# Normalising the second attention's first inputs early, and applying its norm weight to the input instead of the weights

## Chip, cores and metric

The kernel runs on one core of a Trainium2 chip. The metric is the device time of one launch in microseconds (us), as the median of several executions. One more execution was recorded by the hardware profiler. Engines are TensorE (PE, with its weight loads PEld), VectorE (DVE), ScalarE (ACT), GpSimd (POOL) and SyncE (SP), which issues the DMAs. They run in parallel, each of them in its own program order, and wait for one another through semaphores.

## The reference

All data is fp32: 16 batches of 512 positions with 512 features. Three blocks follow one another for each batch: a cross-attention with 16 heads over 77 keys and a norm behind it, a mamba2 block with a residual (its output is `h`), and a second cross-attention with 8 heads of 64 over the same 77 context rows and a norm before it. The change is in the last one:

```python
h = _mamba2_block(x, ...)
xn = (h - mean(h)) * rsqrt(var(h) + EPS) * ln_w + ln_b     # per row of 512
q = (xn @ Wq).reshape(b, Lq, 8, 64)
k, v = enc @ Wk, enc @ Wv                                   # 77 keys
p = softmax(where(pad_mask, -1e9, q k^T / 8))
out = h + (p @ v) @ Wo
```

`ln_w` and `ln_b` are vectors of 512, neither constant nor zero in the data.

## The kernel before, in words

**Stages.** The keys and values of both attentions are made first. Then PhaseA does the first attention of all batches, PhaseB the mamba blocks and PhaseC the second attention. Results between stages lie in DRAM. PhaseB has 8 units of work a batch (n = 128, one for each 128 of the 1024 inner channels) and PhaseC 4 (n = 64, one for each pair of heads). The last drain of PhaseB (`rest`, five units) is interleaved with PhaseC's weights (`setup`) and its first units (`lead`, units -14 to -1) in `tile_kernel`, L1590 to L1615.

**Order.** Each engine's order is that of the program text: PE, DVE, ACT and POOL are scheduled by hand all through, SP inside PhaseB's units. Every unit is a list of steps in which each step works for a unit some lags ahead or behind, so that a step's input has been made some units earlier. In PhaseC (`unit`, L1444) a lag of -5 means: for the unit five later.

**Precision.** A full-precision product is three matmuls (`mm3`, L36 to L38) on operands split into a rounded high part and the rest: names end in h and l. Splitting is one cast on ACT and one subtraction on another engine.

**PhaseB around the change.** `prepare` (L873) normalises, transposes and stores the next batch's input, within the units of the current one; the last batch has no next one. `turn_x1` (L856) is the DVE block transpose. The tiles for this (tag x8, two buffers) are thus free in the last batch.

**PhaseC, one unit.** In the order of the text: `turn_p` (L1406, DVE block transpose `pb` of the probabilities, then a DMA), `finish` (L1439, DVE adds the residual: `hr`), `soft_exp` (L1384, eight ACT exponentials), `qproj` (PE, 12 matmuls), `scores` (L1370, four matmuls; DVE adds the padding, `sc`, and takes the maximum, `mx`), `soft_div` (L1390: DVE reciprocal `sm`, POOL product `sc`), `query` (L1366, ACT moves `q` out of PSUM and adds the bias `bq`), `load_xT` (DMA of transposed input `xf`), `split_x` (L1353, ACT cast `nh`, POOL subtraction `nl`), in two of four units `norm` (L1332, two ACT activations `ht`) and `turn_x` (L1337, two DVE transposes `xb`), in another one `store_x` (L1343), `stats` (L1319, DVE mean and variance of one row block), in one of four units `rstd` (L1327: 12 small DVE operations `c_ve`, `c_y`, `c_t`, then two on POOL, `nm`), `attend` (L1416, PE; ACT cast `ct1h`, DVE subtraction `ct1l`), `project` (PE). So `h` is loaded 14 units ahead, normalised 9 ahead, stored transposed to DRAM, loaded back 6 ahead and split 5 ahead.

**The norm's weight and bias** are put into the query weights once: `setup` (L1264) loads Wq, computes `bq` = ln_b Wq with 16 matmuls of one column, scales Wq's rows by ln_w on DVE (L1292), and splits Wq; then Wo is split in four pieces (`split_piece` L126, `stream` L145), one in `setup` and three while the first units run.

```python
def split_x(self, b, k):
    xf = self.XF.pop((b, k))
    xh, xl = self.X[b, k] = pair(self.p1, [P, S], "n", bufs=8)
    self.nc.scalar.copy(xh, xf)
    self.nc.gpsimd.tensor_sub(xl, xf, xh.bitcast(F32))
```

Of the kernel before, what the change touches and what calls it, by code (L numbers as in the profile page):

```python
# [8 lines left out]
F32 = mybir.dt.float32  # L9
FR = mybir.dt.float32r  # L10
U8 = mybir.dt.uint8
AF = mybir.ActivationFunctionType
# [706 lines left out]
class PhaseB:  # L719


    def __init__(self, g):
        self.g, self.nc = g, g.nc
        self.n = 8 * g.nb
        self.drain = False
        self.Bt, self.Ut = {}, {}
        seq = []
        for i in range(self.n):
            if i % 8 == 0 and i == 0:
                seq += [16, 17]  # L730
            seq += [8 + i % 8, i % 8]
            if i % 8 == 7 and i + 1 < self.n:
                seq += [16, 17]
        self.wseq = iter(seq)
        self.wq = []
# [137 lines left out]
    def prepare(self, b, step):  # L873

        if step in (1, 2):
            self.scale_x1((0, 1) if step == 1 else (2, 3))
        if step in (2, 3):
            for m in (0, 1) if step == 2 else (2, 3):
                self.turn_x1(m)
        if step == 4:  # L880
            self.store_x1(b)
        if step == 5:
            self.load_xT(b)

    def head_x(self, b, k):
        nc, o = self.nc, self.Bt[b]
# [247 lines left out]
    def unit(self, i, side=iter(())):  # L1134


        n, nb = self.n, self.g.nb
        cur, prev, prev2 = (divmod(i - q, 8) if 0 <= i - q < n else None for q in range(3))

        def tail(lag):  # L1140
            b, q = divmod(i - lag, 8)
            return (b, q % 4, q >= 4) if i >= lag and b < nb else (0, 0, None)

        tb, tm, late = tail(6)
        eb, em, elate = tail(7)
        nxt = i // 8 + 1 if i % 8 == 7 and i // 8 + 1 < nb else None
        first = cur and cur[1] == 0
        more = i // 8 + 1 if i // 8 + 1 < nb else None
        k = i % 8
        if more and k == 0:  # L1150
            self.load_x1(more)
        if prev:
            self.tokens(*prev)
        if nxt:
            self.head_turn(nxt)
        if elate:
            self.tail_end(eb, em)
        if prev2:
            self.gate(*prev2)
        if prev:  # L1160
            self.weigh(*prev)
            self.decay(*prev)
        if cur:
            self.projx(*cur)
            if i:
                self.load_decay(*cur)
            self.convx(*cur)
        if i == 0:
            self.head_decay(0)
            self.store_decay(0)  # L1170
            self.load_decay(0, 0)
        next(side, None)
        if nxt:
            self.head_steps(nxt)
        if elate:
            self.tail_store(eb, em)
        if prev:
            self.steps(*prev)
        if nxt:
            self.projz(*cur)  # L1180
            self.head_x(nxt, 2)
            self.head_x(nxt, 3)
        next(side, None)
        if late is not None:
            self.Bt[tb].ps = self.out_half(tb, tm, 4 * late)
        if first:
            self.head_silu(cur[0])
        if late is False:
            part = self.o2.tile([P, D], F32, name="part", bufs=4)
            self.nc.scalar.copy(part, self.Bt[tb].ps)  # L1190
            self.Bt[tb].part.append(part)
        if prev:
            self.states(*prev)
        if k == 2 and i >= 10:
            self.tail_norm(i // 8 - 1)
        if late:
            self.tail_pre(tb, tm)
        if prev2:
            self.gate_split(*prev2)
        if cur:  # L1200
            self.silux(*cur)
            if not nxt:
                self.projz(*cur)
        if prev:
            self.load_ecs(*prev)
        if first:
            self.head_bt(cur[0])
        next(side, None)
        if prev:
            self.intra(*prev)  # L1210
        if more and k in (1, 2, 3, 4, 5):
            self.prepare(more, k)
        if nxt:
            self.head_bc(nxt, 0)
        next(side, None)
        if first:
            self.head_g(cur[0])
        if prev:
            self.inter(*prev)
        if more and k == 6:  # L1220
            self.head_dt(more)
            self.head_x(more, 0)
            self.head_x(more, 1)
        if nxt:
            self.head_decay(nxt)
            self.head_bc(nxt, 1)
            self.store_decay(nxt)
        lb, lm, llate = tail(5)
        if llate:
            self.tail_load(lb, lm)  # L1230
# [8 lines left out]
class PhaseC:  # L1239
# [24 lines left out]
    def setup(self):  # L1264

        g, nc, wp = self.g, self.nc, self.wp
        nc.scalar.preload_act_table_set("natural_log_exp_and_others")
        lw = wp.tile([P, KT], F32, name="lw")
        nc.sync.dma_start(lw, col_view(g.i["L1_ca_ln_w"]))
        lb = wp.tile([P, KT], F32, name="lb")  # L1270
        nc.sync.dma_start(lb, col_view(g.i["L1_ca_ln_b"]))
        self.kb = [wp.tile([P, KT, 2 * NK], F32, name=f"kc{j}") for j in range(2)]
        for j in range(2):
            nc.gpsimd.memset(self.kb[j], 0.0)
        self.padb = wp.tile([P, NK], F32, name="padb")
        nc.gpsimd.tensor_scalar(self.padb, g.padf, -1e9, 0.0, op0=ALU.mult, op1=ALU.add)
        self.wq = pair(wp, [P, KT, 512], "wq1")
        self.wo = pair(wp, [P, KT, 512], "wo1")
        self.bq = wp.tile([P, KT], F32, name="bq1")
        raws = [self.p1.tile([P, 512], F32, name="wr", bufs=6) for k in range(KT)]  # L1280
        for k in range(KT):
            nc.sync.dma_start(raws[k], g.i["L1_Wq"][k * P:(k + 1) * P, :])
        yield
        pbq = bank(g, "w")
        for t in range(KT):
            for k in range(KT):
                nc.tensor.matmul(pbq[:, t:t + 1], raws[k][:, t * P:(t + 1) * P], lb[:, k:k + 1],
                                 start=k == 0, stop=k == KT - 1)
        yield
        nc.vector.tensor_copy(self.bq, pbq[:, :KT])  # L1290
        for k in range(KT):
            nc.vector.tensor_scalar(raws[k], raws[k], lw[:, k:k + 1], None, op0=ALU.mult)  # L1292
            if k % 2:
                yield
        for k in range(KT):
            nc.scalar.copy(self.wq[0][:, k, :], raws[k])
            nc.vector.tensor_sub(self.wq[1][:, k, :], raws[k], self.wq[0][:, k, :].bitcast(F32))
            if k % 2:
                yield
        pieces = [split_piece(g, *self.wo, k, g.i["L1_Wo"], (self.p1, "wr", 6)) for k in range(KT)]  # L1300
        for _ in stream(pieces, 2):
            yield

    def load_h(self, b, m):
# [46 lines left out]
        self.nc.sync.dma_start(t_, self.g.xt1[b % 2][k * P:(k + 1) * P, :])  # L1351

    def split_x(self, b, k):  # L1353
        xf = self.XF.pop((b, k))
        xh, xl = self.X[b, k] = pair(self.p1, [P, S], "n", bufs=8)
        self.nc.scalar.copy(xh, xf)
        self.nc.gpsimd.tensor_sub(xl, xf, xh.bitcast(F32))

    def qproj(self, b, t):
        nc, wq = self.nc, self.wq  # L1360
# [4 lines left out]

    def query(self, b, t):  # L1366
        q = self.Q[b, t] = self.p1.tile([P, S], F32, name="q1")
        self.nc.scalar.activation(q, self.QP.pop((b, t)), AF.Identity, bias=self.bq[:, t:t + 1])

    def scores(self, b, t):  # L1370
        nc, q, kb = self.nc, self.Q.pop((b, t)), self.kb[b % 2]
# [72 lines left out]
    def unit(self, i):  # L1444


        def at(lag, f, *a):
            if 0 <= i - lag < self.n:
                f(*divmod(i - lag, 4), *a)

        last = i - 3 >= self.n - 2
        at(-14, self.load_h)
        if i % 4 == 1:
            at(-3, lambda b, t: self.load_k(b))
        if i % 4 == 0:
# [11 lines left out]
        at(-5, self.split_x)  # L1467
        if i % 4 in (3, 0):
            for m in (0, 1) if i % 4 == 3 else (2, 3):
                at(-9, lambda b, t: self.norm(b, m))  # L1470
                at(-9, lambda b, t: self.turn_x(b, m))
        if i % 4 == 1:
            at(-7, lambda b, t: self.store_x(b))
        at(-13, self.stats)
        if i % 4 == 2:
            at(-10, lambda b, t: self.rstd(b))
        at(4, self.attend)
        at(8, self.project)

    def lead(self):  # L1480
        for i in range(-14, 0):
            self.unit(i)
            yield

# [9 lines left out]
def tile_kernel(ctx: ExitStack, tc, ins, out, phases="kabc", dbg=None):  # L1494
# [28 lines left out]
    ctx.enter_context(tc.manual_schedule(engines={E.PE, E.DVE, E.Activation, E.Pool}))  # L1523
    nc.scalar.preload_act_table_set("natural_log_exp_and_others")
    A, B, C = PhaseA(g) if "a" in phases else None, PhaseB(g), PhaseC(g)

    def consts():
        nc.sync.dma_start(pad8, bcast_rows(ins["pad"][0]))
# [61 lines left out]
    if "c" in phases:  # L1590
# [4 lines left out]
            for _ in range(n):  # L1595
                next(it, None)

        step(lead, 3)
        step(setup)
        step(lead, 2)  # L1600
        step(rest)
        step(lead, 2)
        step(rest)
        for _ in range(3):
            step(setup, 2)
            step(rest)
            step(lead)
        step(lead, 4)
    for _ in rest:
        pass  # L1610
    if "b" in phases:
# [43 lines left out]
```

## Time and profile before

| what | value |
|---|---|
| median of 3 runs | 3018.6 us (3016.53 to 3019.37) |
| profiled execution | 3013.72 us, its span 3011.9 us |
| busy: PE / DVE / ACT / POOL | 2867.6 / 2406.4 / 1825.5 / 1473.1 us |
| share of the span | 95% / 80% / 61% / 49% |
| granted PE clock, mean | 0.985 |
| DMA, HBM read and written | 445.10 MB and 129.42 MB, 191 GB/s |
| last mamba batch | 2346 to 2446 us |
| transition: drain, setup, first units | 2446 to 2555 us |
| second attention | from 2498.42 us (first `sc`) to the end |

An engine's busy time is the sum of its instructions. A row of the timeline gives start, duration, engine, line, operation, output<-input and count, and in brackets the engine's idle time before it with what ended that. A row of the waits gives waiting operation <- what it waited for, the sum in us, how often, and the longest one. Starts of successive rows tell what an instruction costs its engine; durations overlap a little.

### The profile page before, as it was taken

How to read it: one execution, taken by the hardware profiler on the slowest of the kernel's cores; microseconds unless marked ns; L12 is line 12 of the kernel's file. 1: busy time of each engine (PE TensorE's matmuls, PEld its weight loads, DVE VectorE, ACT ScalarE, POOL GpSimd, SP SyncE). 2: the span in 40 equal slices, each digit the busy share in tenths (PEclk: the TensorE clock that was granted, in tenths of full speed). 3: DMA queues.
4: the chain of work that ended last, by engine and by line, in shares of the span. 5: the costliest groups of instructions: out<-in, count | busy, mean ns of one | idle time of the engine just before them, and what ended most of it. 6: DMA issues, size and time to landing. Idle time of an engine off the chain costs nothing.

```text
span 3011.9 us, 47659 instructions
## 1 busy us (share of the span) xinstructions
PE 2867.6 (95%) x15712; PEld 2144.9 (71%) x15712; DVE 2406.4 (80%) x3875; ACT 1825.5 (61%) x4970; POOL 1473.1 (49%) x1106
## 2 busy tenths in 40 slices
PE   9999999997799999999999999999999988999999
PEld 7755555554677877877787787778778765777776
DVE  4267888887878988988898898889889887777764
ACT  3256666664665666566666656666665647666663
POOL 1036666665665555555555555555555543333331
PEclk9999999998899999999999999999999988999999
DMA  7345555545566756665665666566566557989874
GB/s 231 92 125 156 164 161 155 158 143 155 172 195 193 224 164 203 213 183 191 195 222 167 202 210 186 188 197 220 171 202 206 169 177 217 267 271 274 269 242 149
DMA packets 421604, 578.22 MB, mean 192 GB/s; under 512 B 105982, under 2 KB 248494, under 8 KB 421358
## 3 DMA queue, kind: packets, MB, share of 16 engines
q1 hardware_dynamic: 421358, 575.18, 62.6%
q8 instruction: 125, 2.05, 0.3%
q14 instruction: 121, 0.99, 0.1%
HBM read 445.10 MB, written 129.42 MB: 191 GB/s over the span
## 4 chain that ended last, share of the span: by engine, by line
PE 53%; DVE 30%; issue 5%; POOL 4%; DMA 4%; ACT 2%; SPq 1%; DVEq 0%; POOLq 0%; ACTq 0%
DVE dbc L1016 6%; PE ps_o L36 5%; PE ps_o L38 5%; PE ps_o L37 5%; PE ps_w L37 4%; DVE dbc L1018 4%; DVE acc L815 4%; PE ps_w L38 4%; PE ps_w L36 4%; PE ps_y L36 3%; PE ps_y L37 3%; PE ps_y L38 3%; POOL nl L889 3%; PE ps_z L1074 2%; DVE sc L360 2%
## 5 line engine op out<-in xcount | busy, mean ns | idle before, releaser
L36 PE MATMUL ps_w<-nh,wb 128*128 128x512 f32 x1152 | 476.5, 414 | 0.3 <-ACT nh L888 0.3
L37 PE MATMUL ps_w<-nl,wb 128*128 128x512 f32 x1152 | 454.6, 395 | 15.9 <-POOL nl L889 15.9
L38 PE MATMUL ps_w<-nh,wb 128*128 128x512 f32 x1152 | 453.3, 394 | 0.0
L1083 POOL TENSOR_TENSOR yt<-yt,ebc 128x384 f32<-128x384 f32 x128 | 225.5, 1762 | 422.8 <-DVE ebc L1082 422.8
L1016 DVE TENSOR_TENSOR_SCAN dbc<-dbc,delta 128x512 f32<-128x512 f32 x256 | 387.0, 1554 | 0.0
L815 DVE SCALAR_TENSOR_TENSOR acc<-ps_w,cw,acc 128x511 f32<-128x511 f32 (+2 forms) x384 | 286.1, 745 | 23.4 <-ACT acc L813 14.4
L1018 DVE TENSOR_TENSOR dbc<-dbc,gm 128x1024 f32<-128x1024 f32 x128 | 272.1, 2125 | 5.5
L37 PEld LDWEIGHTS ps_w<-nl,wb 128*128 128x128 f32 x1152 | 218.3, 189 | 64.8 <-POOL nl L889 28.2
L1090 POOL TENSOR_TENSOR gl<-yt,gh 128x512 fp32r<-128x512 f32 x128 | 170.5, 1332 | 185.9 <-ACT gh L1089 180.2
L1084 POOL TENSOR_TENSOR yt<-yt,sz 128x512 f32<-128x512 f32 x128 | 254.9, 1991 | 10.0
L38 PEld LDWEIGHTS ps_w<-nh,wb 128*128 128x128 f32 x1152 | 216.9, 188 | 47.8
L36 PEld LDWEIGHTS ps_w<-nh,wb 128*128 128x128 f32 x1152 | 218.1, 189 | 41.1 <-issue 2.6
L1393 POOL TENSOR_TENSOR sc<-sc,sm 128x616 f32<-128x616 f32 x64 | 78.6, 1229 | 295.3 <-DVE sm L1392 263.9
L1044 ACT ACTIVATE u<-ps_x,dt 128x64 f32<-128x64 f32 x1024 | 221.9, 333 | 0.0
L1035 ACT ACTIVATE wu<-ps_x,et 128x64 f32<-128x64 f32 x768 | 170.9, 323 | 68.6 <-PE ps_x L1026 68.6
L813 ACT ACTIVATE acc<-ps_w,cb,cw 128x512 f32<-128x512 f32 x128 | 99.8, 780 | 176.7 <-PE ps_w L38 176.7
L360 DVE TENSOR_TENSOR sc<-ps_s,mt 77x2048 f32<-77x2048 f32 x64 | 145.1, 2267 | 71.8 <-PE ps_s L358 71.5
L36 PE MATMUL ps_o<-woph,gh 128*128 128x512 f32 x496 | 196.4, 396 | 0.0
L37 PE MATMUL ps_o<-wopl,gh 128*128 128x512 f32 x496 | 196.2, 396 | 0.0
L38 PE MATMUL ps_o<-woph,gl 128*128 128x512 f32 x496 | 196.2, 396 | 0.0
L1388 ACT ACTIVATE sc<-sc,mx 128x77 f32<-128x77 f32 x512 | 176.7, 352 | 0.2 <-DVE mx L1381 0.2
L889 POOL TENSOR_TENSOR nl<-xf,nh 128x512 fp32r<-128x512 f32 x64 | 101.0, 1600 | 125.4 <-ACT nh L888 125.4
(331 smaller groups left out, 7414.4 us busy)
## 6 DMA issues: line engine op xcount, KB each, us to landing
wb<-win SPq DMA_DIRECT2D x288, 512.0 KB
dbc<-dec SPq DMA_DIRECT2D x128, 512.0 KB
ebc<-ecs SPq DMA_DIRECT2D x256, 96.0 KB
pt<-pb SPq DMA_DIRECT2D x62, 384.0 KB
xt<-in_xT_dram SPq DMA_DIRECT2D x64, 256.0 KB
xb<-in_x_dram SPq DMA_DIRECT2D x64, 256.0 KB
x<-xb SPq DMA_DIRECT2D x64, 256.0 KB
xf<-x1t SPq DMA_DIRECT2D x16, 1024.0 KB
```

The costliest lines, as they stand in the source:

```text
L36: nc.tensor.matmul(ps, ah, bh, start=start, stop=False)
L37: nc.tensor.matmul(ps, ah, bl, start=False, stop=False)
L38: nc.tensor.matmul(ps, al, bh, start=False, stop=stop)
L360: nc.vector.tensor_mul(sc, ps[:NK], mt[:, None, :].to_broadcast((NK, 4, S)))
L815: nc.vector.scalar_tensor_tensor(acc[:, s:], ps[:, :S - s], cw[:, j, 3 - s:4 - s], acc[:, s:], op0=ALU.mult, op1=ALU.add)
L889: nc.gpsimd.tensor_sub(hl, o.xf[:, k, :], hh.bitcast(F32))
L1016: nc.vector.tensor_tensor_scan(flat, flat, self.delta.rearrange("p c i -> p (c i)"), 0.0, op0=ALU.mult, op1=ALU.add)
L1018: nc.vector.tensor_mul(lm, lm, o.gm[:, None, :, :].to_broadcast((P, 2, 4, P)))
L1044: nc.scalar.activation(w.u[:, c, h, :], w.pu[:, f:f + 64], AF.Copy, scale=o.dtc[:, c, 2 * t + h:2 * t + h + 1])
L1083: nc.gpsimd.tensor_add(yt[:, P:], yt[:, P:], t2)
L1084: nc.gpsimd.tensor_mul(yt, yt, w.sz)
L1388: self.nc.scalar.activation(sc[:, h, :], sc[:, h, :], AF.Exp, bias=mx[:, h:h + 1], accum_out=sm[:, h:h + 1])
```

## The change

**Early batches.** A new function `next_stage` of PhaseB is called nine times in the last mamba batch (units 120 to 128), for batches 0 and 1 of the second attention: it loads the whole `h` of the batch (1 MB), makes mean and variance on DVE (4 + 4 operations), the reciprocal deviation (12 small DVE operations, 2 on POOL), normalises on ACT (4), transposes on DVE (4), and stores by four DMAs to the place where `store_x` would. PhaseC leaves these steps out for its first 8 units (`done = 8`), and `lead` starts at unit -6 instead of -14.

**Weight and bias.** Wq is no longer scaled and there is no `bq`; Wq and Wo are split alike in a stream of eight pieces with four loads ahead (four pieces in the transition, four with the first units). Instead `split_x` multiplies each loaded `xf` by ln_w and adds ln_b in place, before the split, on DVE for batch 0 and on POOL for the other 15. `query` becomes a plain ACT copy.

**Order.** `setup`, `lead` and `rest` are interleaved anew, with SP's order by hand there too.

```diff
+    def next_stage(self, k):
+        g, nc, p2 = self.g, self.nc, self.p2
+        b, k = divmod(k, 4)
+        if k == 0 and b > 0:
+            x = self.XB.rearrange("p j m r -> p j (m r)")
+            dst = g.xt1[b - 1].rearrange("(j s) (a n) -> a s j n", s=32, n=P)
+            for a in range(4):
+                nc.sync.dma_start(dst[a], x[32 * a:32 * a + 32])
+        if b == 2:
+            return
+        if k == 0:
+            self.XN = p2.tile([P, KT, D], F32, name="xn", tag="x8")
+            nc.sync.dma_start(self.XN, g.h[b].rearrange("(m p) d -> p m d", p=P))
+        if k == 1:
+            self.HM = p2.tile([P, KT, 2], F32, name="hm", bufs=1)
+            for m in range(KT):
+                s6 = p2.tile([P, 6], F32, name="hs")
+                nc.vector.bn_stats(s6, self.XN[:, m, :])
+                nc.vector.bn_aggr(self.HM[:, m, :], s6)
+        if k == 2:
+            rs = rstd_bits(g, p2, self.HM[:, :, 1], [P, KT], "h")
+            nm = neg_mean(g, p2, self.HM[:, :, 0], rs, [P, KT], "hn")
+            for m in range(KT):
+                x = self.XN[:, m, :]
+                nc.scalar.activation(x, x, AF.Identity, scale=rs[:, m:m + 1], bias=nm[:, m:m + 1])
+        if k == 3:
+            for m in range(KT):
+                self.turn_x1(m)
...
+        if self.ahead and 0 <= i - n + 8 <= 8:
+            self.next_stage(i - n + 8)
...
-        pbq = bank(g, "w")
-        for t in range(KT):
-            for k in range(KT):
-                nc.tensor.matmul(pbq[:, t:t + 1], raws[k][:, t * P:(t + 1) * P], lb[:, k:k + 1],
-                                 start=k == 0, stop=k == KT - 1)
...
-            nc.vector.tensor_scalar(raws[k], raws[k], lw[:, k:k + 1], None, op0=ALU.mult)
...
+        pieces = [split_piece(g, *w, k, g.i[n], (self.p1, "wr", 6))
+                  for w, n in ((self.wq, "L1_Wq"), (self.wo, "L1_Wo")) for k in range(KT)]
+        for _ in stream(pieces, 4):
             yield
...
     def split_x(self, b, k):
-        xf = self.XF.pop((b, k))
+        nc, xf = self.nc, self.XF.pop((b, k))
         xh, xl = self.X[b, k] = pair(self.p1, [P, S], "n", bufs=8)
-        self.nc.scalar.copy(xh, xf)
-        self.nc.gpsimd.tensor_sub(xl, xf, xh.bitcast(F32))
+        e = nc.gpsimd if b else nc.vector
+        e.tensor_scalar(xf, xf, self.lw[:, k:k + 1], self.lb[:, k:k + 1], op0=ALU.mult, op1=ALU.add)
+        nc.scalar.copy(xh, xf)
+        nc.gpsimd.tensor_sub(xl, xf, xh.bitcast(F32))
...
-        self.nc.scalar.activation(q, self.QP.pop((b, t)), AF.Identity, bias=self.bq[:, t:t + 1])
+        self.nc.scalar.copy(q, self.QP.pop((b, t)))
...
-        at(-14, self.load_h)
+        todo(-14, self.load_h)
...
-        at(-13, self.stats)
+        todo(-13, self.stats)
...
-        for i in range(-14, 0):
+        for i in range(self.done and -6 or -14, 0):
...
-        step(lead, 3)
-        step(setup)
-        step(lead, 2)
-        step(rest)
-        step(lead, 2)
-        step(rest)
-        for _ in range(3):
+        with tc.manual_schedule(engines={E.SP}):
+            step(setup)
+            step(lead)
+            step(rest)
+            step(setup)
+            step(lead)
+            step(rest)
             step(setup, 2)
+            step(lead)
             step(rest)
             step(lead)
-        step(lead, 4)
+            step(lead)
+            step(rest)
+            step(lead)
+            step(rest)
+            step(lead, 14)
```

More of the change, by code (lines that the diff above doesn't have):

```diff
@@ L726, in __init__ @@
         self.Bt, self.Ut = {}, {}
+        self.ahead = False
         seq = []
@@ L1267, in setup @@
         nc.scalar.preload_act_table_set("natural_log_exp_and_others")
[L1268 to L1271, printed above, removed]
+        self.lw = wp.tile([P, KT], F32, name="lw")
+        nc.sync.dma_start(self.lw, col_view(g.i["L1_ca_ln_w"]))
+        self.lb = wp.tile([P, KT], F32, name="lb")
+        nc.sync.dma_start(self.lb, col_view(g.i["L1_ca_ln_b"]))
         self.kb = [wp.tile([P, KT, 2 * NK], F32, name=f"kc{j}") for j in range(2)]
@@ L1278, in setup @@
         self.wo = pair(wp, [P, KT, 512], "wo1")
-        self.bq = wp.tile([P, KT], F32, name="bq1")
-        raws = [self.p1.tile([P, 512], F32, name="wr", bufs=6) for k in range(KT)]
-        for k in range(KT):
-            nc.sync.dma_start(raws[k], g.i["L1_Wq"][k * P:(k + 1) * P, :])
-        yield
-        pbq = bank(g, "w")
-        for t in range(KT):
-            for k in range(KT):
-                nc.tensor.matmul(pbq[:, t:t + 1], raws[k][:, t * P:(t + 1) * P], lb[:, k:k + 1],
-                                 start=k == 0, stop=k == KT - 1)
-        yield
-        nc.vector.tensor_copy(self.bq, pbq[:, :KT])
-        for k in range(KT):
-            nc.vector.tensor_scalar(raws[k], raws[k], lw[:, k:k + 1], None, op0=ALU.mult)
[L1293 to L1301, printed above, removed]
+        pieces = [split_piece(g, *w, k, g.i[n], (self.p1, "wr", 6))
+                  for w, n in ((self.wq, "L1_Wq"), (self.wo, "L1_Wo")) for k in range(KT)]
+        for _ in stream(pieces, 4):
             yield
@@ L1449, in at, with todo @@
                 f(*divmod(i - lag, 4), *a)
+        def todo(lag, f, *a):
+            if i - lag >= self.done:
+                at(lag, f, *a)
         last = i - 3 >= self.n - 2
-        at(-14, self.load_h)
+        todo(-14, self.load_h)
         if i % 4 == 1:
@@ L1469, in unit @@
             for m in (0, 1) if i % 4 == 3 else (2, 3):
-                at(-9, lambda b, t: self.norm(b, m))
-                at(-9, lambda b, t: self.turn_x(b, m))
+                todo(-9, lambda b, t: self.norm(b, m))
+                todo(-9, lambda b, t: self.turn_x(b, m))
         if i % 4 == 1:
-            at(-7, lambda b, t: self.store_x(b))
-        at(-13, self.stats)
+            todo(-7, lambda b, t: self.store_x(b))
+        todo(-13, self.stats)
         if i % 4 == 2:
-            at(-10, lambda b, t: self.rstd(b))
+            todo(-10, lambda b, t: self.rstd(b))
         at(4, self.attend)
@@ L1525, in tile_kernel @@
     A, B, C = PhaseA(g) if "a" in phases else None, PhaseB(g), PhaseC(g)
+    B.ahead = "b" in phases and "c" in phases
+    C.done = 8 if B.ahead else 0
     def consts():
```

## The prediction

> **What bounds the kernel now.** The page puts TensorE (PE) at 95% of a span of 3011.9 us, but that is an average over stages, so I read the windows by stage first (columns: length, then busy time of PE, weight loads, DVE, ACT, POOL; granted PE clock; DMA share).
>
> ```profile
> 2346.00:2446.00 100.00, 96.17 (x597) 79.70 (x596) 91.63 (x128) 59.39 (x181) 57.38 (x35) 1.00 0.55 176
> 2446.00:2555.00 109.00, 83.49 (x338) 62.11 (x337) 86.24 (x207) 62.75 (x205) 37.76 (x44) 0.83 0.68 206
> 2555.00:2900.00 345.00, 345.00 (x1596) 255.76 (x1594) 268.81 (x571) 230.47 (x882) 113.45 (x110) 1.00 0.90 268
> ```
>
> Last mamba batch: PE 96% and DVE 92%, so both are nearly full. Transition: PE idle for 25.5 us of 109. Second attention: PE never idle, DVE 78%, POOL 33%. The waits between 2560 and 2950 show what order POOL, ACT and DVE stand in there:
>
> ```profile
> POOL sc L1393 <- DVE sm L1392: 206.7, 44, 5.3
> ACT q L1368 <- PE ps_y L38: 103.4, 48, 2.5
> DVE sc L1378 <- PE ps_w L1377: 77.0, 39, 2.6
> ```
>
> POOL's `sc` is always released by DVE's reciprocal; DVE's `sc` by PE. ACT's `nh` (L1356) waits only 8.2 us in all, for its DMA: today nothing that DVE or POOL makes is read by it. One unit (7.81 us of PE) with a normalisation in it, on DVE, ACT and POOL:
>
> ```profile
> 2641.36 1.01 DVE L1378 TENSOR_TENSOR sc<-ps_w,padb 128x308 f32<-128x308 f32 x2 [0.17 <-PE ps_w L1377]
> ...
> 2643.12 0.20 DVE L1392 RECIPROCAL sm<-sm 128x8 f32<-128x8 f32 x1
> 2643.23 1.26 DVE L94 STREAM_TRANSPOSE xb<-ht 128x512 f32<-128x512 f32 x2
> ...
> 2645.19 0.66 DVE L1425 TENSOR_TENSOR ct1l<-ps_z,ct1h 128x512 fp32r<-128x512 f32 x1
> 2645.76 0.97 DVE L94 STREAM_TRANSPOSE pb<-sc 128x768 f32<-128x768 f32 x1
> 2646.66 0.65 DVE L1441 TENSOR_TENSOR hr<-ps_o,hr 128x512 f32<-128x512 f32 x1
> 2649.17 1.00 DVE L1378 TENSOR_TENSOR sc<-ps_w,padb 128x308 f32<-128x308 f32 x2 [1.86 <-PE ps_w L1377]
> ```
>
> ```profile
> 2641.49 0.61 ACT L1356 CAST nh<-xf 128x512 fp32r<-128x512 f32 x1
> 2641.99 1.52 ACT L1335 ACTIVATE ht<-ht,nm,c_y 128x512 f32<-128x512 f32 x2
> 2643.42 0.57 ACT L1424 CAST ct1h<-ps_z 128x512 fp32r<-128x512 f32 x1
> ```
>
> ```profile
> 2643.39 1.23 POOL L1393 TENSOR_TENSOR sc<-sc,sm 128x616 f32<-128x616 f32 x1 [4.79 <-DVE sm L1392]
> 2644.58 1.30 POOL L1357 TENSOR_TENSOR nl<-xf,nh 128x512 fp32r<-128x512 f32 x1
> ```
>
> `nh` starts 1.6 us before the reciprocal, so `ht` is ready when DVE turns it. DVE has 1.86 us to spare in this unit.
>
> **Part 1, second attention: a new wait.** In program order, POOL's new scaling of `xf` stands behind the `sc` product and before `nl`; `nh` must follow it, and on ACT `ht` and `ct1h` stand behind `nh`; on DVE the turn of `ht`, the statistics, `ct1l`, `pb`, `hr` and the next `sc` stand behind those. So DVE's reciprocal starts a chain POOL, ACT, DVE that must end before DVE's next reciprocal. The scaling of this shape is in the trace once:
>
> ```profile
> L831 POOL TENSOR_SCALAR praw<-praw,fr 128x512 f32<-128x512 f32 x4 | 2.8, 691 | 0.0
> ```
>
> It is on the path: 0.74 us with the handoff. Start to start, from the rows above and their like: reciprocal to product 0.27, product to its successor 1.19, scaling 0.74, `nh` to `ht` 0.50, `ht` to statistics 2.19 (two casts, second turn), to `ct1l` 0.79, `pb` 0.57, `hr` 0.90, `sc` 0.57, `mx` 0.89, next reciprocal 0.71: 9.32 us for a unit with `ht`. Without `ht`, `ct1h` follows `nh` and `ct1l` follows that by 0.60: 6.94. The unit with the rstd chain has its own DVE work, 7.9 to 8.3 (at most the present 2658.73 to 2667.05). Four units: 2 x 9.32 + 6.94 + 7.9 to 8.3 = 33.5 to 33.9, against PE's 4 x 7.81 = 31.24. Excess 2.3 to 2.65 us a batch; units 9 to 54 still normalise, 11.5 batches: +26 to +30, I take **+28**. POOL also now waits for `xf`'s DMA with the next product behind it: the 8.2 us of waits become POOL's; taken at 0 more (0 to 5).
>
> [...] DVE's scaling of the same shape (L1292) takes 0.88 us for two, some 0.45 each. [...]
>
> **Part 2, the first units.** Units 1 to 8 are short today (2502.58 to 2555.49, 6.6 each), as no projection is running. With the same sum less the operations not yet there, units 4, 5, 7, 8 go from 6.78, 5.06, 6.34, 6.65 to 8.75, 6.4, 8.6, 8.75: +7.7. A fourth piece of Wo (0.6) and `wo1l` behind `nh` in units 1 and 2 (1.5): **+10** (5 to 12).
>
> **Part 3, last mamba batch.** Twice: 4 statistics 3.2, rstd chain 2.35, 4 transposes 2.45 = 8.0 us, so 16 us more on DVE in units 120 to 127. DVE is idle 5.5 us there. So +10 us of delay of everything behind it (bounds +5, if the batch's end frees some; +16, if no gap is used). ACT's 4 + 4 activations (5.8 us) and POOL's 4 small operations lie in idle time (ACT 59%, POOL 57%); if not, they lengthen ACT's chain by under 2. SP: two 1 MB loads, two stores of four DMAs. The store of batch 0 stands in unit 124 and waits for the last transpose of unit 123, with the decay loads of the next unit behind it; DVE does that transpose before it needs those, so 0 (0 to 2). DMA share is 0.55; 4 MB in 100 us is 40 GB/s on 176.
>
> [...]
>
> ```profile
> 2659.73 0.52 DVE L55 TENSOR_SCALAR c_ve<-mv 128x4 f32<-128x4 f32 x1
> 2660.29 1.21 DVE L57 TENSOR_SCALAR c_y<-c_ve 128x4 int32<-128x4 int32 x1
> ```
>
> [...] I take the rows, and keep +10 for the high end.
>
> **Part 4, transition.** Removed: 16 matmuls of bq (4.62 us PE and a wait of 0.63), 4 DVE scalings, statistics and transposes of two batches, and this wait:
>
> ```profile
> 2480.24 0.79 PE L36 MATMUL ps_y<-nh,wq1h 128*128 128x512 f32 x1 [9.51 <-ACT nh L1356]
> ```
>
> DVE also stood 7.07 us at 2496.23 (`ht` behind an `nh` waiting for `xf`) before the first `sc` at 2498.42. After: mamba's last matmul ends at 2480.24 - 9.51 - 5.25 = 2465.5; plus 10.1 from part 3, 2475.6; two query projections, 6.3 each (12 matmuls: 4.8 at 0.40, 7.4 today with waits), and 1 us of scores: first `sc` at 2489.2 instead of 2498.4: **-9** (-19 with no delay from part 3, -3 with 16 us). Next late is the mamba drain on DVE, not a DMA. Wq's loads stand behind the store of batch 1 on SP, about 2447, and are needed at 2475: 0.
>
> **Sum.** -9 + 10 + 28 = +29. The profiled run took 3013.72 (span plus 1.8) and the median is 3018.6, 0.16% above; I add to the median: 3047.6.
>
> **Rivals.**
> (a) Not slower: the chain hides. It decides only if four units pass 31.24 us. For: POOL is 67% idle, PE runs some work ahead of DVE. If a unit with `ht` stays under 8.2 (the turn of `ht` and the product overlapping better than their starts today), parts 1 and 2 are 0 and the result is 3018.6 - 9 = 3009.6. Against: all those steps are in fixed order on each engine.
> (b) The backlog takes the gain: part 3 at 16 us, part 4 at -3, chain at +5: 3020.
> [...]
> (d) The rows for the next stage aren't ahead of use: excluded, since h of batches 0 and 1 was stored more than ten batches earlier.
>
> **Chances.** Forecast 0.60 (3036 to 3056), (c) 0.22, (a) 0.12, (b) 0.06. About 0.2% (6 us) is what a measurement can tell from no change: faster 0.12, same 0.06, slower 0.82. The range runs from 3016 to 3068: it leaves (a) below and little above.
>
> **What would show it.** In 2555 to 2900: PE below 95%, `ht` waited for by DVE's `xb` and `nh` by POOL's scaling, unit starts 8.4 us apart on average. Last batch: DVE without a gap, PE idle 10 us more. Transition: no PE wait of 9.5 on `nh`. Wrong would be PE still at 345 of 345, or POOL's scaling well off 0.7 us, or a first `sc` before 2480 or after 2500.

## The result and the profile after

The changed kernel takes 3064.15 us (median of 4 runs, 3059.99 to 3068.94), the kernel before 3017.57 (4 runs): ratio 1.0158, 95% interval 1.0145 to 1.0171, so +46.6 us, slower. The forecast was +29 (3047.6), the range 3016 to 3068. The profiled run's span is 3064.3, 52.4 above before.

First the same windows of the changed kernel (same columns; the borders are moved with the stages):

```profile
2346.00:2456.00 110.00, 102.24 (x597) 82.32 (x595) 103.80 (x174) 65.54 (x197) 55.78 (x38) 1.00 0.55 174
2456.00:2555.00 99.00, 73.45 (x296) 53.71 (x297) 64.50 (x147) 47.69 (x161) 43.31 (x49) 0.83 0.65 200
2555.00:2952.00 397.00, 364.89 (x1627) 268.16 (x1627) 277.71 (x584) 229.41 (x911) 152.93 (x158) 0.97 0.78 235
```

In the second attention PE is busy for 364.89 of 397 us (92%), where it had no gap before; DVE falls from 78% to 70% busy. No engine is full any more: they wait for one another in a ring, DVE for ACT, ACT for POOL, POOL for DVE. The waits from 2560 to 2955 name it:

```profile
POOL sc L1408 <- DVE sm L1407: 202.2, 46, 6.0
ACT nh L1371 <- POOL xf L1370: 167.4, 45, 5.0
DVE xb L94 <- ACT ht L1348: 80.9, 23, 4.1
```

DVE's `sc` waited for PE for 77.0 us before; that is 3.4 us now, and PE waits for DVE's `ct1l` and `hr` instead (17.6 and 7.6 us).

Where the 52.4 us arise can be read from marks in both traces. The mark at the start is PE's column sum (`ps_x<-ones,sqa`) that closes the batch before the last mamba batch. There the changed one's profiled run is already 5.0 us late (2380.60 against 2375.61). Only four of the added operations stand before the mark (the statistics of batch 0, 3.2 us of DVE from 2371.50), and DVE's row `yt<-xs,dsk,ps_y` ahead of them is as late (2351.47 against 2346.44); the other kernels with the same early work have the mark at 2370.22 to 2375.54. So the 5.0 us are variation between runs, and part 3 is measured from the mark on.

| stretch | before | after | difference | forecast |
|---|---|---|---|---|
| start to mark | 2375.61 | 2380.60 | +5.0 | 0 |
| mark to next column sum (last mamba batch) | 76.86 | 87.83 | +11.0 | +10 |
| mark to DVE's first reciprocal | 128.57 | 122.61 | -6.0 | -9 |
| first to tenth reciprocal (units 1 to 9) | 60.87 | 74.78 | +13.9 | +10 |
| tenth to 55th (45 units) | 351.30 | 391.21 | +39.9 | +28 |
| 55th to the end | 95.5 | 95.1 | -0.4 | 0 |

The second row is contained in the third. The sum of the last four is 47.4 us, close to the 46.6 of the medians.

### The profile page after: what moved, and what is told of

Read it like the earlier page. It is cut to its first block, busy times and chain, and to the rows that moved or that the text cites. A ratio compares the mean times of both kernels' runs of the same rounds, so it can differ in the third digit from the quotient of the medians.

```text
span 3064.3 us, 47625 instructions
## 1 busy us (share of the span) xinstructions
PE 2883.7 (94%) x15680; PEld 2149.1 (70%) x15680; DVE 2402.1 (78%) x3874; ACT 1815.9 (59%) x4970; POOL 1522.0 (50%) x1166
## 4 chain that ended last, share of the span: by engine, by line
PE 52%; DVE 23%; issue 10%; POOL 7%; DMA 4%; ACT 3%; SPq 1%; DVEq 0%; POOLq 0%; ACTq 0%
PE ps_w L37 6%; PE ps_w L38 6%; PE ps_w L36 6%; PE ps_o L36 5%; PE ps_o L37 4%; PE ps_o L38 4%; DVE dbc L1047 3%; PE ps_z L1105 3%; POOL nl L920 3%; PE ps_y L1098 3%; DVE acc L816 2%; DVE dbc L1049 2%; DVE sc L360 2%; PE ps_x L1082 2%; PE ps_y L36 2%
## 5 line engine op out<-in xcount | busy, mean ns | idle before, releaser
L1371 ACT CAST nh<-xf 128x512 fp32r<-128x512 f32 x64 | 39.7, 620 | 227.5 <-POOL xf L1370 211.9
```

## Experiments

All kernels stood beside runs of the kernel before on the same chip. Its median there was 3013.7 (first four), 3013.3 (next four) and 3012.3 (last three), 4 to 5 us under that of the result, and the expectations were written with the result's level in mind; so differences are compared.

| kernel | median, us | to before | ratio, 95% interval |
|---|---|---|---|
| changed kernel | 3064.15 | +46.6 | 1.0158 (1.0145 to 1.0171) |
| e1_order | 3008.63 | -5.1 | 0.9981 (0.9974 to 0.9988) |
| e2_dve | 3024.79 | +11.1 | 1.0037 (1.0026 to 1.0049) |
| e3_early_only | 3007.28 | -6.4 | 0.9980 (0.9973 to 0.9987) |
| e4_scale_only | 3067.62 | +53.9 | 1.0180 (1.0161 to 1.0198) |
| e5_preload | 3004.42 | -8.9 | 0.9972 (0.9964 to 0.9981) |
| e6_preload_lag7 | 2999.72 | -13.6 | 0.9958 (0.9944 to 0.9972) |
| e7_double | 3096.21 | +82.9 | 1.0281 (1.0266 to 1.0297) |
| e8_no_stats | 3001.91 | -11.4 | 0.9964 (0.9951 to 0.9977) |
| e9_tile | 3009.95 | -2.4 | 0.9998 (0.9986 to 1.0009) |
| e10_store_early | 3009.14 | -3.2 | 0.9993 (0.9982 to 1.0004) |
| e11_nh_last | 3026.73 | +14.4 | 1.0051 (1.0034 to 1.0068) |

The theory: the place of the scaling in POOL's order closes a ring DVE, POOL, ACT, DVE that is longer than PE's unit. The rivals: the added work itself costs, which would leave e1_order near the changed kernel's time, or the early normalisation does.

**e1_order**, the same instructions with one of them moved in `unit`:

```diff
+    def scale_x(self, b, k):
+        nc, xf = self.nc, self.XF[b, k]
+        e = nc.gpsimd if b else nc.vector
+        e.tensor_scalar(xf, xf, self.lw[:, k:k + 1], self.lb[:, k:k + 1], op0=ALU.mult, op1=ALU.add)
...
     def split_x(self, b, k):
-        e = nc.gpsimd if b else nc.vector
-        e.tensor_scalar(xf, xf, self.lw[:, k:k + 1], self.lb[:, k:k + 1], op0=ALU.mult, op1=ALU.add)
...
+        at(-5, self.scale_x)
         at(1, self.soft_div)
```

> The same instructions as the changed kernel; only POOL's scaling of xf stands before the product with the reciprocal instead of behind it. Chain theory: xf is there before, so nh no longer waits for the reciprocal (start to start 2.29 us in the changed kernel), units return to 7.81 us, the 39 us of units 10 to 54 and most of the 14 us of the first units go: 3064 - 39 - 8 = 3017, between 3010 and 3022. [...]

Measured: -5.1 us to before, 51.7 below the changed kernel. Its waits from 2560 to 2950:

```profile
POOL xf L1369 <- DMA xf<-xt: 102.3, 42, 4.9
POOL sc L1411 <- DVE sm L1410: 96.9, 42, 5.3
ACT q L1386 <- PE ps_y L38: 79.8, 42, 2.4
DVE sc L1396 <- PE ps_w L1395: 57.8, 32, 2.6
ACT nh L1374 <- POOL xf L1369: 40.6, 27, 4.9
```

Now the scaling waits for its DMA, and DVE and ACT wait for PE again. POOL does as much as in the changed kernel, and the 45 units take 351.4 us, against 391.2 there and 351.3 before. So the place in the order is what costs, which decides against the first rival. In e5_preload, with the same work on POOL, they take 348.7 us, which is PE's pace (7.75 us each); so the work itself costs nothing there.

**e2_dve**: `nc.vector.tensor_scalar(xf, ...)` for all batches, in the place where the change has it.

> The scaling of xf on DVE for all batches. Chain theory: a unit with ht becomes reciprocal 0.11, scaling 0.46, then nh and the rest 7.2 = 7.8 us, equal to PE's 7.81; the excess over PE is 0 to 0.5 us a batch: 3017 to 3025. Rival (any added work on DVE or POOL costs here): DVE gets 60 times 0.46 = 28 us more, so about 3017 + 28 - 9 = 3036 or more.

Measured: +11.1, 35.5 below the changed kernel. The ring is shorter with DVE in POOL's place: units with `ht` take 7.78 us when `xf` is there. But when it isn't, DVE itself stands and everything of DVE behind it: the DMA wait is no longer hidden (in most batches the first unit with `ht` takes 8.95 to 10.33 us; DVE's scaling at 2671.17 waited 1.33 us for `xf`). My 3017 to 3025 was -1 to +7 to before; this is some 4 us beyond, so a miss, and less than the rival's +18.

**e3_early_only**: `setup`, `split_x` and `query` as before (with `bq`), early normalisation and SP's new order kept.

> Early normalisation of batches 0 and 1 alone, with weight and bias in Wq and bq as before. Chain theory: no new wait in the second attention; the last mamba batch is 7 to 16 us longer, the transition gains about as much less 5 us for bq: 3014 to 3024. Rival (the early work is what costs): 3050 or more.

**e4_scale_only**: the reverse, the kernel before with the changed `setup`, `split_x` and `query`.

> The kernel before with weight and bias applied to the input (POOL from batch 1 on) and the order of the changed kernel in that step, no early normalisation. Chain theory: 39 us in units 10 to 54, up to 14 in the first ones, less up to 6 us for bq and the scaling of Wq: 3055 to 3068. Rival (the early work costs): 3010 to 3020.

Measured: -6.4 and +53.9. The sum of both, +47.5, is close to the result (+46.6). Against the level of the result the expectations were some -4 to +6 and +37 to +50, so each is missed by 2 to 4 us, on the side away from its rival. The early normalisation alone is a small gain, so the second rival falls; the loss comes with the scaling.

**e7_double**, more of the suspected cost:

```diff
         e.tensor_scalar(xf, xf, self.lw[:, k:k + 1], self.lb[:, k:k + 1], op0=ALU.mult, op1=ALU.add)
+        if b:
+            e.tensor_scalar(xf, xf, self.one, self.zero, op0=ALU.mult, op1=ALU.add)
```

> The changed kernel with a second scaling (by one, plus zero) behind the first on POOL from batch 1 on. Chain theory: 0.75 us more in each of the three units of a batch in which the chain sets the pace, up to four: 11.5 batches x 2.3 to 3.0 us = 26 to 35, plus 4 to 6 in the first units: 3064 + 30 to 41 = 3094 to 3105. Rival (POOL has idle time for it): under 3070.

Measured: +82.9 to before, 36.3 more than the changed kernel, within the expected +30 to +41. A batch's four units went from 9.43, 9.42, 7.11, 8.67 to 10.28, 10.29, 7.96, 9.12: each 0.85 us longer, one 0.45 (the rstd unit, which partly hides it). The second scaling adds 0.87 us to POOL from start to start, so in those three units POOL's time counts in full.

**e11_nh_last**, another link of the ring opened: POOL's order as in the change, `nh` and `nl` moved behind `attend`, so that `ht` and `ct1h` no longer stand behind them on ACT.

> The changed kernel with POOL's order kept, but nh and nl moved behind ht and ct1h in the program. Chain theory: DVE's turn of ht and ct1l no longer stand behind POOL's scaling; the ACT exponentials then start some 2.9 us after the reciprocal and end before the next one, so units are PE-bound: 3006 to 3014. Rival (POOL's scaling behind the product is late for nl or for the query projection itself): 3040 or more.

Measured: +14.4, which neither the 3006 to 3014 nor the rival's 3040 foresaw. Units with `ht` are at 7.79 to 7.82, so the link was the right one: they took 9.43 us because `ht` and `ct1h` stood behind `nh`. I had not seen what was next late. In the rstd unit POOL's `nl` now stands behind the two `nm` operations, which wait for DVE's rstd chain, and PE waits for `nl` (11 times, 9.5 us in all); the unit takes 8.95:

```profile
2668.47 0.50 PE L37 MATMUL ps_y<-nl,wq1h 128*128 128x512 f32 x1 [0.87 <-POOL nl L1375]
```

By the marks, the transition gains 5.6 us on before, the first units lose 8.3 (69.1 us from first to tenth reciprocal) and the 45 units after them 12.5, or 1.1 a batch, which the rstd unit makes.

**e8_no_stats** (e1_order, `k == 1` left out and `k == 2` an ACT copy) sizes part 3.

> e1_order, leaving out the statistics, the rstd chain and the normalisation's scale and bias of the two early batches (ACT copies x onto itself instead). Takes 11 us off DVE in the last mamba batch. If that DVE work is on the path, the stretch between the last two PE sums (88.4 us in e1_order, 76.9 before) shrinks to 77 to 79 and the run to 2998 to 3001; if DVE's gaps hide it, less than 3 us.

The stretch between the column sums fell from 88.43 to 78.16 us, as expected, in two parts. DVE's last product of the batch (`dbc`) ends 7.4 us sooner behind the mark, so 7.4 of the 11 us were on the path. PE's matmuls from there to the column sum take 8.56 us at a granted clock of 1.00, where they took 11.45 at 0.73 in e1_order: the other 2.9. By the medians the run gained only about 6 (-11.4 against -5.1 to before), less than the 8 to 11 expected. The first query projection starts 11.5 us sooner and lasts 11.7 us to the start of the second instead of 10.9; that takes back under 1 us. In the profiled execution the first reciprocal comes 10.8 us sooner behind the mark. Why the medians show less stays open.

**e5_preload** shortens the wait of the first query projection. Two of the loads of batch 0's `xf` stood on SP behind stores of `h`, which wait for the drain.

```diff
             step(setup)
+            for k in range(KT):
+                C.load_xT(0, k)
```

> e1_order with the four loads of batch 0's xf issued right behind Wq's loads, ahead of the drain's stores of h on SP. If the first query projection is spread over 10.9 us (2473.39 to 2484.32 in e1_order) because two of its xf loads stand behind those stores, it takes about 5.5 us and the run is 4 to 5 us below e1_order: about 3004. Rival (DVE's share in the drain sets it): no change from 3008.6.

Measured: -8.9, 3.8 better than e1_order; the projection takes 6.98 us instead of 10.93, and the first reciprocal comes 3.9 us sooner behind the mark. That is nearly the 4 to 5 expected.

**e6_preload_lag7** (each later `xf` also a unit earlier, `at(-7, self.load_xT)`) and **e10_store_early** (that with the store a unit earlier). In the first, the load of a batch's first row block stands before the store that fills it, so this block is of an older batch; its time is that of a schedule with one dependence missing.

> e5_preload with every later xf loaded one unit earlier too. In e1_order POOL waits 102 us in all for xf's DMA and units vary from 6.6 to 9.8 us; if these waits reach PE, another 2 to 4 us go: 3000 to 3002. Rival (PE's work ahead covers them): same as e5_preload within 1.5 us.

> e6_preload_lag7 with the transposed store one unit earlier, so that it stands before the first of its loads in the program, as in the changed kernel (e6_preload_lag7 had that load before its store, so that a quarter of its xf was of an older batch). If nothing new is late: 2999 to 3002. If SP, which waits for the transposes with other loads behind it, is late with pT or hr: 3003 to 3008.

Measured: -13.6 and -3.2, the second beyond both of its alternatives (3009.1). In e6_preload_lag7 POOL's waits for `xf` are gone, but from the tenth to the 55th reciprocal both it and e5_preload take 348.7 us: there, PE's work ahead had covered them, as the rival says. The 4.7 us come from the first units (60.5 against 63.9 us from first to tenth reciprocal) and the stage before, and with a dependence missing. With it in place (e10_store_early) the 45 units take 355.5 us, 6.8 more; the store, which waits for DVE's transposes, then stands ahead of more loads on SP, but that this is what is late was not shown. e5_preload stays the best one with the whole computation, 0.28% faster than before (interval 0.19% to 0.36%).

## Why the prediction was right, and where its sizes were off

**Part 1, the ring, was right in kind and too small.** A unit with `ht` after, by engine: DVE, ACT, POOL.

```profile
2665.36 0.19 DVE L1407 RECIPROCAL sm<-sm 128x8 f32<-128x8 f32 x1
2669.02 1.42 DVE L94 STREAM_TRANSPOSE xb<-ht 128x512 f32<-128x512 f32 x2 [3.47 <-ACT ht L1348]
...
2674.79 0.19 DVE L1407 RECIPROCAL sm<-sm 128x8 f32<-128x8 f32 x1
```

```profile
2667.65 0.62 ACT L1371 CAST nh<-xf 128x512 fp32r<-128x512 f32 x1 [3.69 <-POOL xf L1370]
2668.18 1.52 ACT L1348 ACTIVATE ht<-ht,nm,c_y 128x512 f32<-128x512 f32 x2
```

```profile
2665.63 1.23 POOL L1408 TENSOR_TENSOR sc<-sc,sm 128x616 f32<-128x616 f32 x1 [5.41 <-DVE sm L1407]
2666.84 0.77 POOL L1370 TENSOR_SCALAR xf<-xf,lw,lb 128x512 f32<-128x512 f32 x1
```

Follow the starts: reciprocal 2665.36, product +0.27, scaling +1.21, `nh` +0.81, `ht` +0.53, `xb` +0.84, and back at the reciprocal after 9.43 us. I had 9.32; the scaling with its handoff is 0.81 instead of 0.74. A unit without `ht` takes 7.11 (6.94 forecast). The term most off is the rstd unit, 8.67 instead of 7.9 to 8.3 (8.32 before): I had thought of the collision at the two TENSOR_SCALARs, and not that POOL's scaling and a later `nl` collide with other operations of the chain.

```profile
2684.80 0.49 DVE L59 TENSOR_SCALAR c_y<-c_y 128x4 f32<-128x4 f32 x1
...
2685.92 0.16 DVE L62 SCALAR_TENSOR_TENSOR c_t<-c_y 128x4 f32<-128x4 f32 x1
2686.11 1.21 DVE L63 TENSOR_TENSOR c_t<-c_t,c_ve 128x4 f32<-128x4 f32 x1
2687.36 0.16 DVE L64 SCALAR_TENSOR_TENSOR c_y<-c_t,c_y 128x4 f32<-128x4 f32 x1
```

```profile
2684.49 0.78 POOL L1370 TENSOR_SCALAR xf<-xf,lw,lb 128x512 f32<-128x512 f32 x1
2686.01 1.30 POOL L1372 TENSOR_TENSOR nl<-xf,nh 128x512 fp32r<-128x512 f32 x1 [0.74 <-ACT nh L1371]
```

A product of 4 elements a row takes 1.21 us, to the end of POOL's `nl`. Before, L57 lost as much beside `nl` (1.21, in the prediction's rows; `nl` from 2660.18 to 2661.47 there), so that loss has only moved; new is L59, 0.49 beside the scaling where it took 0.17 before. Both long operations end with POOL's: L63 at 2687.32 and `nl` at 2687.31, L59 at 2685.29 and the scaling at 2685.27. L63 at 2685.52, with nothing on POOL, took 0.16, and in e11_nh_last, where `nl` comes after the chain, all of L63 take 0.16 to 0.17. Not every operation is longer there: L57 at 2684.57 took 0.20 beside the scaling. Why was not shown.

So a batch is 34.6 us (8.67, 9.43, 9.42 and 7.11), an excess of 3.4 instead of 2.3 to 2.65. Ten full batches of this make 34.0 of the 39.9 us, the last five units 1.4; the prediction had counted 11.5 batches. The other 4.5 come from five late units that it did not have: three without `ht` at 8.2 us (the PE clock, at the end of this document) and two with `ht` at 9.92 and 10.05, where POOL's scaling waited 0.5 and 0.6 us for the DMA of `xf`, the wait put at 0 to 5 us in all.

**The two rows of a scaling.** Taking POOL's own row, L831 (0.69 us), and not DVE's 0.45 was right: 60 scalings on POOL took 782 ns on average. POOL's work beside DVE was not the main cause (e1_order has the same work there and no loss); what it cost DVE is in the rows above.

**Part 2** was +13.9 against +10. Units 4, 5, 7 and 8 made 8.9 (7.7 forecast), the same ring with the same shortfall; the others made 5.0, 2.8 of them in unit 1, where the 2.1 for the pieces of Wo was too small: DVE's `wo1l` at 2506.66 waited 2.49 us for a cast of ACT that stood behind `nh`.

**Part 3** gave +11.0 against +10, in part by luck. DVE's work delays its `dbc` by 8.7 us, as gaps took 7.3 of the 16 us and not 5.5 (it ends at 2457.36, 76.8 us behind the mark, and ended at 2443.64, 68.0 behind). The rest is a term that the prediction did not have: from there to the column sum PE took 10.81 us instead of 8.57, at a granted clock of 0.78 instead of 1.00 (columns as above, before and then after):

```profile
2443.90:2452.47 8.57, 7.84 (x47) 5.96 (x47) 7.59 (x16) 2.92 (x4) 7.01 (x7) 1.00 0.66 241
2457.62:2468.43 10.81, 10.06 (x46) 7.88 (x46) 2.00 (x6) 3.75 (x6) 7.02 (x7) 0.78 0.87 291
```

PE had waited 4.34 us just before, and 2.11 us in the kernel before. e1_order is like the one (4.38 us, clock 0.73), e8_no_stats like the other (2.47 us, clock 1.00).

**Part 4** gave -6.0 for -9; 1 us of this is part 3. The step that failed is that "next late is the mamba drain on DVE, not a DMA". PE's own waits there after:

```profile
2483.65 0.79 PE L36 MATMUL ps_y<-nh,wq1h 128*128 128x512 f32 x1 [2.90 <-ACT nh L1371]
...
2487.93 0.80 PE L36 MATMUL ps_y<-nh,wq1h 128*128 128x512 f32 x1 [1.72 <-ACT nh L1371]
```

`nh` waits for DVE's scaling, and that for the DMA of `xf` (1.89 and 2.92 us). SP issues the third and fourth of these loads, at 2478.45 and 2482.21, only behind stores of `h`, which wait for DVE's drain:

```profile
2479.45 0.32 SPq L1163 DMA_DIRECT2D h<-xr  x1
...
2482.21 0.59 SPq L1364 DMA_DIRECT2D xf<-xt  x1
```

So the drain counted here by way of SP's queue. The first projection took 12.2 us (2478.12 to 2490.30) instead of 6.3; in e1_order (10.9 us), e5_preload gave 4 of them back by the order of the loads alone.

**The signs.** PE fell to 92%, `xb` waited for `ht` and `nh` for the scaling, and PE's wait of 9.5 us was gone, as forecast. Units were 8.7 us apart instead of 8.4. In the last mamba batch PE's idle time grew by 5.6 us (2.8 to 8.4 between the column sums), not by 10. One reading of the kernel before was too strong: POOL's `sc` was released by the reciprocal in 44 of 50 waits, not always.

**Rivals.** (a) asked whether four units pass 31.24 us: 34.6. Of (b) nothing was seen, part 3 being 11 us and not 16. The measured 3064.15 lies in the range but above the 3036 to 3056 that had the chance of 0.60, and it is the very number of (c), about 3064. That is a coincidence: no run shows its terms. The scaling took 0.78 us and not 1.0, part 3 was 11 us and not 16, and in place of the +10 for the high end stretched operations of DVE made some 0.3 us a batch. The time is near the high end since parts 1, 2 and 4 erred the same way, by 12, 4 and 3 us.

## What to carry to other kernels

What an instruction costs on an engine with idle time depends on its place in that engine's order: ask what stands before it there, what that waits for, and whether the result feeds the engine where the wait began. Here the same 60 instructions cost some 50 us behind a product and at most a few ahead of it; once in the ring, more length there counted almost in full (e7_double). When a path is freed, look at the issuing queue for what is late next.

## What the runs showed of the hardware that was not expected

**A 16-byte tile.** Six of the kernels without the `bq` tile (e1, e2, e5, e6, e8 and e10) ran PE-bound units in 7.75 us instead of 7.81. One row each of the query matmul between 2700 and 2800 of e1_order, then of e9_tile, which allocates this tile again and reads it nowhere:

```profile
L36 PE MATMUL ps_y<-nh,wq1h 128*128 128x512 f32 x51 | 19.8, 389 | 0.0
```

```profile
L36 PE MATMUL ps_y<-nh,wq1h 128*128 128x512 f32 x51 | 20.2, 397 | 0.0
```

> e1_order with the small bq tile allocated again (set to zero, not read). PE-bound units took 7.81 us before and in e3_early_only, 7.75 in the kernels without bq, with query matmuls of 394 to 396 against 389 to 391 ns. If the 16 bytes that move the later tiles make that, units return to 7.81 us and the run is 3 us longer than e1_order; if Wq's values or the missing bias make it, they stay at 7.75.

Its units are 7.82 us again, and its ratio to before is 0.9998 where e1_order had 0.9981: an unread tile is enough, without the scaled Wq or the bias. The expectation is wrong in that not all kernels without `bq` are fast: e4_scale_only, e7_double and e11_nh_last, which allocate or order other tiles differently, have matmuls of 395 ns too. All this fits with where the later tiles lie, but that it is the address is inferred; which address is good was not tried.

**The PE clock after short waits.** In the changed kernel PE waited 1.13 and 0.38 us shortly after one another (at 2671.86 and 2673.32), and eight matmuls from 2674.13 on then started 0.43 us apart instead of 0.23. One batch earlier it waited 1.17 and 0.38 us in the same places, and nothing of the kind followed. Rows of the one, then of the other:

```profile
2673.32 0.50 PE L36 MATMUL ps_o<-wo1h,ct1h 128*128 128x512 f32 x1 [0.38 <-DVE hr L1456]
...
2674.13 0.63 PE L36 MATMUL ps_o<-wo1h,ct1h 128*128 128x512 f32 x1
```

```profile
2638.69 0.50 PE L36 MATMUL ps_o<-wo1h,ct1h 128*128 128x512 f32 x1 [0.38 <-DVE hr L1456]
...
2639.48 0.40 PE L36 MATMUL ps_o<-wo1h,ct1h 128*128 128x512 f32 x1
```

Of 19 such pairs of waits between 2577 and 2955 (0.34 to 1.18 us and then 0.38), five were followed by slow matmuls. The granted clock is 0.52 from 2674 to 2676 and was 1.00 from 2639 to 2642; over this stage it is 0.97 against 1.00 before. In part 3 slow matmuls (0.43 us apart from 2461.83 on) came after one wait of 4.34 us; here they followed 1.3 to 1.6 us in two parts five times, and did not follow as long waits in other batches. What decides it was not shown. The slow matmuls make three of the units without `ht` late (8.2 us in place of 7.1, DVE waiting for PE); the pairs of waits come from the ring.
